# Where a batch's masks stand in the load queue, and where their conversions and sums stand on two engines

## The chip, the cores and the metric

The kernel runs on one core of one Trainium2 chip. The metric is device time in microseconds. The kernel before took 418.82, 419.46 and 419.88 us in three runs, a median of 419.46 us. A core has a matrix engine (TensorE, PE in the profile), a vector engine (VectorE, DVE), a scalar engine (ScalarE, ACT), GpSimd (POOL) and a queue that issues DMAs (SyncE, SP); ScalarE and GpSimd issue DMAs too. Each takes its own instructions in a fixed order.

## The reference, cut to what matters

```python
# first layer, each batch b of 8, 256 tokens of 1024 features
output = jnp.einsum('bsi,oi->bso', hidden_states, W) + b
sign = (2 * mask - 1).astype(hidden_states.dtype)
diff = jnp.einsum('bsi,bio->bso', hidden_states, sign)
x = x + output + diff * coeff[:, None, None]
# second layer: one shared W, and an adapter of rank 16 for each batch
base_out = jnp.einsum('bti,oi->bto', x, W) + b
lora_h = jnp.einsum('bti,bir->btr', x, A)
lora_out = jnp.einsum('btr,bro->bto', lora_h, Bm)
x = x + base_out + lora_out * SCALING
```

Each batch has an integer mask of 1024 x 1024. The first layer's weight of a batch is the shared weight, plus the identity (for the residual), plus the mask times 2c, minus c. All is float32.

## The kernel before

The eight batches are worked in two groups of four: first layer of batches 0 to 3, second layer of these four together, first layer of batches 4 to 7, second layer of those. Activations lie transposed (features on partitions).

**First layer.** A mask is loaded in eight pieces (`load`, L170) of 512 KB, each into a tile `w`, along with four tiles `x` of 256 KB. `build` (L219) turns a piece into a weight: a conversion on ScalarE (L231: times 2c, minus c) and a sum with the shared weight on VectorE (L234). Batches 3 to 7 (`SEVEN`) use a scheme with seven products of half-sized matrices instead of eight. `Seven.operands` makes its operands in 20 steps: the a11 and a12 pieces, two sums of token halves (t1, t2), then a22, a21 and the weight sums s1, s2 (L345), then t3, s3, s4, t4. `Seven.products` runs the seven products: X(a11), Y(a12), X(s2), Z(s1), X(s3), Z(s4), X(a22), each in two halves of 16 matmul instructions (L408), in PSUM banks X, Y, Z. Some results are read from PSUM with the bias on ScalarE (`with_bias`, four reads of L427), others are added on VectorE (`add`, L432). A bank that is accumulated further waits for its read. `Sevens.run_one` hands out operand steps about ten ahead of the products, so conversions and sums of the next batch fall among the reads and additions of the running one.

**Second layer.** `second_layer` runs seven outer products in the order A11, A12, S1, S2, S4, S3, A22 (`plan`). Each is again seven small products, on "leaves" of the weight: a11, s1, s2, a12, s3, a22, s4, of 256 KB each. Leaves are loaded by `load_leaves` on the SP queue. The leaf pool has seven buffers, so a leaf's load waits until an earlier leaf has been used. `run` (one outer product) calls `load_leaves` for the next outer product and starts its first small product X(a11) before the last two of its own. VectorE makes the right operands (T, L856, and their sums, L672 to L678), reads PSUM (L759) and adds the quarters of the result (L842); ScalarE copies the first reads (L757) and the adapters' results (L731). Work laid "beside" a run is taken in between: the sums of the next operands, the remaining leaves of the group's own weight, and `next_weights(n)`, which lets the first `n` operand steps of the next group's batch be built.

**Order.** A scheduler fixes the order of instructions on each engine when the program is built. `tc.issue_after(ins)` keeps what is recorded in it behind `ins` in that order. `behind(name)` does so with the latest instruction kept in `anchors` under that name: "leaves" is the last leaf load, "weights" the last weight sum or addition. `next_masks(n)` (L860) loads the first `n` pieces of the next group's first batch, here batch 4, behind the leaves that are queued at that point. The SP queue takes its loads in order.

Of the kernel before, what the change touches and what calls it, by code (L numbers as in the profile page):

```python
# [11 lines left out]
AF = mybir.ActivationFunctionType  # L12
# [12 lines left out]
def kernel(  # L25
# [38 lines left out]
    nc = tc.nc  # L64
# [42 lines left out]
    two_c = const.tile([P, B], F32, tag="two_c", name="two_c")  # L107
    nc.vector.tensor_scalar_mul(two_c, c_ps, 2.0)
    neg_c = const.tile([P, B], F32, tag="neg_c", name="neg_c")
# [26 lines left out]
    x_sb, weff, raw, weff_at = {}, {}, {}, {}  # L136
    anchors = {}
# [3 lines left out]
    pieces = [(0, None, c) for c in range(NC)]  # L141
    pieces += [(b, h, g) for b in range(1, B) for h, g in (by_seven if b in SEVEN else by_half)]

    def pair(name):
        return qpool.tile([P, 2, CG, OQ], F32, tag="q", name=name)

    def parts(k: int):

        return [slice(i, i + 1) for i in range(2)] if k < BY_HALF else [slice(0, 2)]
# [6 lines left out]
    def w0_of(k: int):  # L156
        b, h, g = pieces[k]
        if b == 0:
            return w0_sb[:, g, :].rearrange("p (h o) -> p h o", h=2)
        return w0_sb[:, g * CG : (g + 1) * CG, h * OH : (h + 1) * OH]  # L160
# [58 lines left out]
    def build(k: int):  # L219

        b, h, g = pieces[k]
        if k == 2 * NG:

            for c in range(NC):
                d = w0_sb[:, c, c * P : (c + 1) * P]
                with tc.issue_after(weff_at[k - 1].ins):
                    nc.vector.tensor_add(d, d, ident)
        w = weff[k]
        m = w.bitcast(I32)
        for i in parts(k):  # L230
            nc.scalar.activation(  # L231
                w[:, i], m[:, i], AF.Identity, bias=neg_c[:, b : b + 1], scale=two_c[:, b : b + 1]
            )
            weff_at[k] = nc.vector.tensor_add(w[:, i], w[:, i], w0_of(k)[:, i])  # L234
            anchors["weights"] = weff_at[k]

    loaded = 0
# [11 lines left out]
    def bank(name):  # L249
        return psum.tile([P, 2, T], F32, tag="ps", name=name)  # L250
# [67 lines left out]
    class Seven:  # L318
# [105 lines left out]
        def with_bias(self, i, v, ps):  # L424
            for j in range(TPH):
                ot = i * TPH + j
                nc.scalar.activation(  # L427
                    self.out(i, v)[:, j, :], ps[:, j, :], AF.Identity, bias=b0_sb[:, ot : ot + 1]
                )

        def add(self, i, v, ps):
            anchors["weights"] = nc.vector.tensor_add(self.out(i, v), ps, self.out(i, v))  # L432

        def products(self):

# [37 lines left out]

    OPERANDS_AHEAD = 10
    FREE_OPERANDS = 7
    def behind(what: str):
        return tc.issue_after(anchors[what].ins) if what in anchors else nullcontext()

    class Sevens:

# [200 lines left out]
    def second_layer(group: int, y, first, first_steps, second):  # L681
# [6 lines left out]
        left_leaf, right = {}, {}  # L688
# [7 lines left out]
        def product(ps, l, r, first=False, by_tile=False):  # L696
            order = [(c, j) for c in range(CG) for j in range(2)]
            if by_tile:
                order.sort(key=lambda cj: cj[1])

            with behind("products") if first else nullcontext(), behind("adapters"):
                for c, j in order:
                    anchors["inner"] = nc.tensor.matmul(  # L703
                        ps[:, j, :],
                        lhsT=l[:, c, j * P : (j + 1) * P],
                        rhs=r[:, c, :],
                        start=first and c == 0 and j == 0,
                        stop=False,
                        skip_group_check=True,
                    )  # L710
# [40 lines left out]
        def begin(n, name, r):  # L751
            banks[n] = bank(f"X_{group}_{n}")
            product(banks[n], left_leaf[name, "a11"], r.b[0, 0], first=True)

        def read(out, ps, other=None):
            if other is None:
                anchors["copies"] = nc.scalar.copy(out, ps)  # L757
                return anchors["copies"]
            own["reads"] = anchors["reads"] = nc.vector.tensor_add(out, ps, other)  # L759
            return anchors["reads"]  # L760

        def store(o, i, j, u, v, c=slice(0, CG), queue=nc.scalar):
            queue.dma_start(outT[GB * group + 2 * j + v, 2 * i + u][:, c], o)
# [3 lines left out]
        def run(n, name, r, seed, out, dest=None, beside=None, early=None, mid=None, late=None, then=None):  # L767

            leaf = {k: left_leaf.pop((name, k)) for k in ("a11", "s1", "s2", "a12", "s3", "a22", "s4")}
            other = seed or {uv: None for uv in UV}
            beside = beside or iter(())
            X = banks.pop(n)

            def done(uv):
                if dest:
                    store(out[uv], *dest, *uv)
                if then:
                    then(uv)  # L780

            read(out[0, 0], X, other[0, 0])
            Z = bank(f"Z_{group}_{n}")
            product(Z, leaf["s1"], r.t["t1"], first=True)
            if early:
                early()
            product(X, leaf["s2"], r.t["t2"])
            next(beside, None)
            read(out[0, 1], X, other[0, 1])
            Y = bank(f"Y_{group}_{n}")  # L790
            product(Y, leaf["a12"], r.b[1, 0], first=True)
            read(out[0, 0], Y, out[0, 0])
            done((0, 0))
            if mid:
                mid()
            if n + 1 == len(plan):
                finish(X, Z, leaf, r, other, out, dest, beside, done)
                return
            product(X, leaf["s3"], r.t["t3"])
            next(beside, None)  # L800
            read(out[1, 1], X, other[1, 1])
            read(out[1, 1], Z, out[1, 1])
            done((1, 1))
            load_leaves(plan[n + 1])
            begin(n + 1, plan[n + 1], right[plan[n + 1]])
            next(beside, None)
            product(X, leaf["a22"], r.t["t4"])
            read(out[1, 0], X, other[1, 0])
            done((1, 0))
            next(beside, None)  # L810
            if late:
                late()
            product(Z, leaf["s4"], r.b[1, 1])
            read(out[0, 1], Z, out[0, 1])
            done((0, 1))
            for _ in beside:
                pass
# [19 lines left out]
        def quads(name):  # L837
            two = [pair(f"{name}{u}_{group}") for u in range(2)]
            return {(u, v): two[u][:, v] for u, v in UV}

        def add(o, x):
            nc.vector.tensor_add(o, o, x)  # L842
# [5 lines left out]
        def outer_sum(n, x, y, name):  # L848


            big_t[n] = [
                tpool.tile([P, TPH, T], F32, tag="T", name=f"T{n}_{group}_{v}") for v in range(2)
            ]
            right[name] = Right(f"T{n}_{group}", big_t[n])
            for v in range(2):
                nc.vector.tensor_sub(big_t[n][v], x[v], y[v])  # L856
                yield
            yield from right[name].sums()

        def next_masks(n):  # L860

            with behind("leaves"):
                if group + 1 < NGROUP:
                    load_to((group + 1) * GB * 2 * NG + n)

        def next_weights(n):
            if group + 1 < NGROUP:
                while sevens[group + 1].made < n:
                    sevens[group + 1].begin(sevens[group + 1].made + 1)
                    yield  # L870


        def ordered(steps):

            while True:
                with behind("reads" if "reads" in own else "layer"):
                    if next(steps, True):
                        return
                yield
# [6 lines left out]
        for _ in ordered(first_steps):  # L886
# [6 lines left out]
            beside=chain(islice(s3, 1), ordered(second.sums()), islice(s3, 4), islice(t1, 2)),  # L893
# [5 lines left out]
        for uv in UV[1:]:  # L899
            add(c11[uv], e1[uv])  # L900
        t2 = ordered(outer_sum(2, b22, big_t[1], "S2"))
        next_masks(4)
        run(
            1, "A12", second, c11, c11,
            dest=(0, 0),
            beside=chain(t1, s3, islice(t2, 2)),
        )
        e5 = quads("e5")
        run(
            2, "S1", right["S1"], None, e5,  # L910
            beside=chain(t2, ordered(right["S4"].sums()), next_weights(2)),
            then=lambda uv: add(c12[uv], e5[uv]),
        )
        run(
            3, "S2", right["S2"], e1, e1,
            beside=ordered(outer_sum(3, b22, b12, "S3")),
            then=lambda uv: add(c12[uv], e1[uv]),
        )
        c21, c22 = quads("c21"), quads("c22")
# [4 lines left out]
            beside=chain(ordered(outer_sum(4, b21, big_t[2], "A22")), next_weights(3)),  # L924
# [169 lines left out]
```

## Time and profile before

| what | us |
|---|---|
| median of three runs | 419.46 |
| the profiled execution, its own time | 420.91 |
| its span, first to last instruction | 419.2 |
| TensorE busy | 404.0 |
| VectorE busy | 312.1 |
| ScalarE busy | 136.6 |
| TensorE's mean granted clock | 0.988 of full |

The span is what the profile divides into shares; the time of the execution is 1.7 us longer. In the profile, a wait is put down to what ended it. The four stages stand at about these places in the span: first layer of batches 0 to 3 until 115 us, second layer of group 0 until 219 us, first layer of batches 4 to 7 until 321 us, second layer of group 1 until the end. Transfers moved 99.56 MB, a mean of 237 GB/s.

### The profile page before, as it was taken

To read this page: it belongs to the slowest core of one execution; us is meant where nothing else is said; L and a number is where in the kernel's file an instruction comes from. 1 tells how busy PE (TensorE), PEld (TensorE's weight loads), DVE (VectorE), ACT (ScalarE), POOL (GpSimd) and SP (SyncE) were. 2 spreads that over 40 slices of the span, in tenths; PEclk is the share of its full clock that TensorE was granted. 3 is DMA by queue.
4 is the path that set the end of the run, shared out by engine and by line. 5 is a ranking of instruction groups with operands and counts; after the bars stand their busy time and mean duration, and the time that the engine had idled before them with its cause. 6 is when DMAs were issued, how large, how long until landed. Compare 5 with 4: busy or idle time off the path is not lost.

```text
span 419.2 us, 6762 instructions
## 1 busy us (share of the span) xinstructions
PE 404.0 (96%) x2554; PEld 360.7 (86%) x2554; DVE 312.1 (74%) x446; ACT 136.6 (33%) x221; POOL 43.0 (10%) x85
## 2 busy tenths in 40 slices
PE   8999999999999399999999899999999999999996
PEld 6888888899968378888889899999999688888885
DVE  3357688999706739997899999999913177898593
ACT  4443625681034001403045864623221330101100
POOL 0000252009750102000000000300000000000000
PEclk9999999999999869999999999999999999999999
DMA  8999999961998949556699948632112237545644
GB/s 291 403 401 398 401 407 412 404 242 43 368 363 276 367 141 299 164 148 210 192 343 406 373 153 306 215 122 62 27 52 65 88 125 231 172 151 160 213 155 151
DMA packets 42404, 99.56 MB, mean 237 GB/s; under 512 B 5636, under 2 KB 6404, under 8 KB 42372
## 3 DMA queue, kind: packets, MB, share of 16 engines
q1 hardware_dynamic: 32690, 76.17, 52.4%
q0 software_dynamic: 4928, 14.71, 9.3%
q10 hardware_dynamic: 4754, 8.26, 5.3%
q8 instruction: 20, 0.33, 0.3%
q14 instruction: 12, 0.10, 0.1%
HBM read 79.19 MB, written 19.92 MB: 236 GB/s over the span
## 4 chain that ended last, share of the span: by engine, by line
PE 77%; DMA 12%; DVE 6%; SPq 1%; ACT 1%; issue 1%; DVEq 0%; ACTq 0%
PE X L703 19%; PE X L408 14%; PE ps L267 13%; PE Z L703 8%; PE Z L408 8%; DMA w<-mask 7%; PE ps L292 4%; PE Y L703 4%; PE Y L408 3%; DMA l_S_a<-leaf_S_a 2%; PE G L721 2%; PE psh L738 2%; DMA w_sb<-w0T 2%; DMA outT<-c 2%; DVE c L842 1%; DVE e L759 1%
## 5 line engine op out<-in xcount | busy, mean ns | idle before, releaser
L231 ACT ACTIVATE w<-w,neg_c,two_c 128x1024 f32<-128x1024 int32 (+1 forms) x67 | 78.9, 1203 | 67.2 <-DMA w<-mask 55.4
L234 DVE TENSOR_TENSOR w<-w,w_sb 128x1024 f32<-128x1024 f32 (+1 forms) x67 | 77.1, 1173 | 25.4 <-ACT w L231 17.5
L267 PE MATMUL ps<-x,w 128*128 128x256 f32 x256 | 55.4, 379 | 0.0
L267 PEld LDWEIGHTS ps<-x,w 128*128 128x128 f32 x256 | 48.6, 190 | 6.6
L427 ACT ACTIVATE y<-X,b_sb 128x128 f32<-128x128 f32 x60 | 17.1, 366 | 58.2 <-PE X L408 58.2
L408 PE MATMUL X<-t,s 128*128 128x128 f32 x288 | 34.0, 276 | 2.0 <-ACT y L427 1.9
L842 DVE TENSOR_TENSOR c<-c,e 128x512 f32<-128x512 f32 x48 | 32.1, 684 | 4.6 <-ACT c L731 4.6
L408 PEld LDWEIGHTS X<-t,s 128*128 128x128 f32 x288 | 32.9, 192 | 2.4 <-ACT y L427 2.4
L731 ACT COPY c<-G 128x512 f32<-128x512 f32 x32 | 16.4, 599 | 49.1 <-PE G L721 33.2
L292 PE MATMUL ps<-x,w 128*128 128x256 f32 x128 | 28.4, 383 | 0.5 <-DVE w L234 0.5
L757 ACT COPY e<-X 128x512 f32<-128x512 f32 x16 | 9.4, 588 | 58.9 <-PE X L703 52.6
L759 DVE TENSOR_TENSOR c<-X,c 128x512 f32<-128x512 f32 (+1 forms) x26 | 16.6, 646 | 16.1 <-PE X L703 16.0
L292 PEld LDWEIGHTS ps<-x,w 128*128 128x128 f32 x128 | 24.6, 193 | 4.3 <-DVE w L234 0.9
L759 DVE TENSOR_TENSOR e<-Y,e 128x512 f32<-128x512 f32 x8 | 5.5, 689 | 25.8 <-PE Y L703 14.0
L703 PE MATMUL X<-T_t,l_S_s 128*128 128x256 f32 x96 | 22.8, 380 | 0.1
L408 PE MATMUL X<-t,w 128*128 128x128 f32 x192 | 22.4, 275 | 0.0
L408 PEld LDWEIGHTS X<-t,w 128*128 128x128 f32 x192 | 21.9, 192 | 0.0
L345 DVE TENSOR_TENSOR s<-w,w 128x1024 f32<-128x1024 f32 x18 | 21.7, 1218 | 0.1
L703 PEld LDWEIGHTS X<-T_t,l_S_s 128*128 128x128 f32 x96 | 18.2, 190 | 2.9 <-DVE e L759 0.5
L703 PE MATMUL X<-T,l_S_a 128*128 128x256 f32 x48 | 12.8, 410 | 7.2 <-DMA l_S_a<-leaf_S_a 7.2
L408 PE MATMUL Z<-t,s 128*128 128x128 f32 x160 | 18.8, 275 | 0.0
L408 PE MATMUL Y<-x,w 128*128 128x128 f32 x160 | 18.7, 275 | 0.0
(144 smaller groups left out, 672.0 us busy)
## 6 DMA issues: line engine op xcount, KB each, us to landing
w<-mask SPq DMA_DIRECT2D x61, 512.0 KB, 7.1
l_S_s<-leaf_S_s SPq DMA_DIRECT2D x32, 256.0 KB, 2.7
x<-xT SPq DMA_DIRECT2D x31, 256.0 KB, 7.0
outT<-c ACTq DMA_DIRECT2D x30, 256.0 KB, 3.0
l_A_s<-leaf_A_s SPq DMA_DIRECT2D x24, 256.0 KB, 2.7
l_S_a<-leaf_S_a SPq DMA_DIRECT2D x24, 256.0 KB, 3.2
w<-w1T SPq DMA_DIRECT2D x16, 256.0 KB, 7.2
leaf_A_s<-A_s POOLq DMA_DIRECT2D x12, 256.0 KB, 6.4
```

The costliest lines, as they stand in the source:

```text
L231: nc.scalar.activation(w[:, i], m[:, i], AF.Identity, bias=neg_c[:, b : b + 1], scale=two_c[:, b : b + 1])
L234: weff_at[k] = nc.vector.tensor_add(w[:, i], w[:, i], w0_of(k)[:, i])
L267: nc.tensor.matmul(ps[j // 2][:, j % 2, :], lhsT=w[:, c, j * P : (j + 1) * P], rhs=x_sb[b, g][:, c, :],  start=first and j % 2 == 0, stop= ...
L292: nc.tensor.matmul(ps[ot // 2][:, ot % 2, :], lhsT=w[:, h, j * P : (j + 1) * P], rhs=x_sb[0, c // CG][:, c % CG, :], start=c == 0 and ot % ...
L345: anchors["weights"] = op(s, self.w[x, a], self.w[y, a])
L408: anchors["products"] = nc.tensor.matmul(ps[:, j, :], lhsT=w[:, c, j * P : (j + 1) * P], rhs=r, start=first and a == 0 and c == 0 and j == ...
L427: nc.scalar.activation(self.out(i, v)[:, j, :], ps[:, j, :], AF.Identity, bias=b0_sb[:, ot : ot + 1])
L703: anchors["inner"] = nc.tensor.matmul(ps[:, j, :], lhsT=l[:, c, j * P : (j + 1) * P], rhs=r[:, c, :], start=first and c == 0 and j == 0, s ...
L731: nc.scalar.copy(dest[b // 2][u, b % 2], ps[b])
L757: anchors["copies"] = nc.scalar.copy(out, ps)
L759: own["reads"] = anchors["reads"] = nc.vector.tensor_add(out, ps, other)
L842: nc.vector.tensor_add(o, o, x)
```

## The change

Three things change. (1) `next_masks(4)` no longer stands ahead of the run of A12 but is split: two pieces of batch 4 after that run, that is behind S1's leaves, and the other two after the run of S1, behind S2's leaves. `next_weights(2)` moves from beside the run of S1 to beside that of S2. (2) `build` records the conversion of a mask behind the latest biased read (`anchors["bias"]`, set in `with_bias`). (3) `build` records the sum of a weight behind the latest addition of a product (`anchors["adds"]`, set in `add`). Where no such anchor is set yet (batches 0 to 2 and the beginning of 3), (2) and (3) do nothing.

```diff
         for i in parts(k):
-            nc.scalar.activation(
-                w[:, i], m[:, i], AF.Identity, bias=neg_c[:, b : b + 1], scale=two_c[:, b : b + 1]
-            )
-            weff_at[k] = nc.vector.tensor_add(w[:, i], w[:, i], w0_of(k)[:, i])
+            with behind("bias"):
+                nc.scalar.activation(
+                    w[:, i],
+                    m[:, i],
+                    AF.Identity,
+                    bias=neg_c[:, b : b + 1],
+                    scale=two_c[:, b : b + 1],
+                )
+            with behind("adds"):
+                weff_at[k] = nc.vector.tensor_add(w[:, i], w[:, i], w0_of(k)[:, i])
             anchors["weights"] = weff_at[k]
...
-                nc.scalar.activation(
+                anchors["bias"] = nc.scalar.activation(
                     self.out(i, v)[:, j, :], ps[:, j, :], AF.Identity, bias=b0_sb[:, ot : ot + 1]
                 )
...
-            anchors["weights"] = nc.vector.tensor_add(self.out(i, v), ps, self.out(i, v))
+            anchors["weights"] = anchors["adds"] = nc.vector.tensor_add(
+                self.out(i, v), ps, self.out(i, v)
+            )
...
         t2 = ordered(outer_sum(2, b22, big_t[1], "S2"))
-        next_masks(4)
         run(
             1, "A12", second, c11, c11,
             dest=(0, 0),
             beside=chain(t1, s3, islice(t2, 2)),
         )
+        next_masks(2)
         e5 = quads("e5")
         run(
             2, "S1", right["S1"], None, e5,
-            beside=chain(t2, ordered(right["S4"].sums()), next_weights(2)),
+            beside=chain(t2, ordered(right["S4"].sums())),
             then=lambda uv: add(c12[uv], e5[uv]),
         )
+        next_masks(4)
         run(
             3, "S2", right["S2"], e1, e1,
-            beside=ordered(outer_sum(3, b22, b12, "S3")),
+            beside=chain(ordered(outer_sum(3, b22, b12, "S3")), next_weights(2)),
             then=lambda uv: add(c12[uv], e1[uv]),
         )
```

More of the change, by code (lines that the diff above doesn't have):

```diff
@@ L142, with behind @@
     pieces += [(b, h, g) for b in range(1, B) for h, g in (by_seven if b in SEVEN else by_half)]
+    def behind(what: str):
+        return tc.issue_after(anchors[what].ins) if what in anchors else nullcontext()
     def pair(name):
@@ L475 @@
     FREE_OPERANDS = 7
-    def behind(what: str):
-        return tc.issue_after(anchors[what].ins) if what in anchors else nullcontext()
     class Sevens:
```

## The prediction

> **What bounds the kernel now.** I read the waits view first, then the chain of waits, then busy time by stretch, and last the timeline with the order of instructions of both kernels. TensorE is busy 404.0 of 419.2 us, so only its gaps and its slow stretches can be won. From the waits view (engine, line, awaited: us in total, times, longest):
> ```profile
> ACT w L231 <- DMA w<-mask: 55.4, 30, 15.1
> ...
> PE X L703 <- DMA l_S_a<-leaf_S_a: 7.2, 1, 7.2
> ...
> PE X L408 <- ACT y L427: 1.9, 1, 1.9
> ```
> Two waits of TensorE can be moved: 7.2 us for one leaf, 1.9 us for one biased read on ScalarE. ScalarE's own 55.4 us for masks costs nothing unless something is queued behind it. The chain of waits (start, us, what) shows both places:
> ```profile
> 137.65 9.68 DMA l_S_a<-leaf_S_a
> 147.33 0.14 issue
> 147.46 8.28 PE X L703 x24
> ...
> 226.57 6.38 DMA w<-mask
> 232.95 0.02 issue
> 232.97 1.24 ACT w L231
> 234.21 1.04 ACT y L427 x4
> 235.25 0.04 issue
> 235.30 3.84 PE X L408 x32
> ```
> First place: the leaf a11 of product S1 is issued at 137.65, behind four masks and four x tiles (132.6 to 137.6; 2 MB + 1 MB), and lands at 147.33. The 24 matmuls after it take 8.28 us, where 24 take 5.18 elsewhere in the chain (347.01). Second place: a bias read (L427) stands on ScalarE behind a conversion (L231) whose mask lands at 232.95, and the next matmul waits for the read. By stretch (columns: PE, PEld, DVE, ACT, POOL busy and count, clock, DMA share, GB/s):
> ```profile
> 137.65:147.46 9.81, 2.61 (x13) 1.98 (x12) 6.44 (x9) 0.00 (x0) 1.29 (x3) 0.77 1.02 390
> 147.46:155.74 8.28, 8.28 (x25) 6.83 (x26) 1.98 (x3) 0.59 (x1) 0.00 (x0) 0.65 0.37 91
> 155.74:176.55 20.81, 20.72 (x97) 17.89 (x95) 20.33 (x30) 6.29 (x7) 2.17 (x4) 1.00 0.78 246
> ...
> 218.90:246.10 27.20, 25.32 (x225) 25.11 (x224) 26.16 (x33) 18.50 (x26) 0.00 (x0) 1.00 0.94 364
> 246.10:271.10 25.00, 25.00 (x226) 25.00 (x225) 24.46 (x34) 14.70 (x25) 2.71 (x5) 1.00 0.62 215
> 271.10:296.50 25.40, 25.29 (x226) 25.10 (x226) 25.40 (x31) 7.96 (x19) 1.58 (x3) 1.00 0.30 95
> ```
> See the DMA share of 1.02 during the stall, the clock at 0.65 after it, and VectorE without a gap afterwards (20.33 of 20.81). The last three lines are batches 4, 5 and 6: 27.2, 25.0 and 25.4 us for the same matmuls. So the stall costs 7.2 + (8.28 - 5.18) = 10.3 us, and batches 4 and 6 hold 2.2 + 0.4 over the clean one: 12.9 us is the most there is.
>
> [...] idle from 140.3, clock 0.50 from 143 to 153, back 5.6 us after work resumed. The gap of 1.9 us left the clock at 1.00. [...]
>
> **The masks' move (L902, and next_weights(2) of L911).** It adds no instruction. In the built order SP now has S1's seven leaves, two masks with two x tiles, S2's leaves, two masks with two x tiles, S4's leaves. Leaf loads wait for a buffer: a11 of S1 for A11's last Z product (133.09 + 1.99, less the overlap: 135.0), then s1, s2, a12 for A12's products ending at 136.6, 138.3, 140.3. With the usual 2.6 to 3.2 us they land at about 138, 139.5, 141.2, 143. TensorE ends Y of A12 at 140.3; its operand T is ready at 139.9 (138.73 + 1.13). One leaf product is 1.73 us (x8 in the chain). The built order then gives: X of S1 140.3 to 142.0; half of Z(s1), whose operand ends at 142.3, to 143.2; X(s3) of A12 to 144.9; the other half 145.8; X(a22) 147.5; Z(s4) 149.3. Before, that Z(s4) ended at 157.5, and S1's X(s2) began at 159.0; now it begins at 149.3. TensorE is 9.7 us early, 8.2 of it in what VectorE follows.
>
> Then VectorE binds. From the read of that Z (157.51) to the read of S4's X (187.09 + 0.68) it works without a real gap: 37 tiles of 128x512 at 0.60 from start to start, five T tiles (L856) and two weight sums (L234) at 1.13 = 22.2 + 5.7 + 2.3 = 30.2 us. The built order has the same instructions, rearranged. From 149.3 they end at 179.5; one read (S2's X after a22, TensorE until 172.9) makes them wait 0.4, so 179.9. S4's X(s3), which needs the last read, begins at 180.0 instead of 188.2: 8.2 us early. After 188.2 TensorE is full for 30.7 us (188.2 to 218.9), SP's waits are for the same products, and all of it shifts.
>
> What can take some back is the masks' new place. The first pair is issued behind S1's s4 leaf (its buffer is free at 145.8) at 146.5 to 148.1, 1.5 MB. A lone mask lands after 4.42 us (207.44 in the chain); at 0.39 MB/us each further 512 KB adds 1.3, so S2's a11 behind it lands at 146.5 + 4.4 + 0.7 + 1.3 + 0.7 + 0.7 = 154.3, or 155.6 if two outT tiles go between. It is wanted at 154.5: 0 to 1.1 us. The second pair, issued at 158.4 after S2's s4, gives S4's a11 at 166.2 against 165.9: 0.3 to 0.5. Behind the leaf there is one VectorE wait of 1.0 (S2's X(s2) waits for a read at 164.2) that covers part. I take 0.7 for both together; the ends are 0 and 3, the latter if each block lands 1.5 late. Stage: 8.2 - 0.7 = 7.5 us. The conversions of these masks on ScalarE (4 of some 1.15) run at about 159 to 165, ahead of the G copies that follow them there at 178; their first two sums on VectorE move from S1's run to S2's (next_weights), inside the 30.2 us, and batch 4 wants them at 210. On SP the S2 leaves also wait for outT stores of A12, four in ScalarE's queue, landing 3.0 after issue: at 153 at the latest, where s1 of S2 is wanted at 159.7. The weights of batch 5 and on do not move on SP.
>
> **The holds (L231 and L234).** No instruction is added and no semaphore of another engine: only the order on ScalarE and VectorE changes, in batches 4 to 7. Count from a batch's first matmul, a product being 3.57 us: X 3.57, Y 7.15, X(s2) 10.7, Z(s1) 14.3, X(s3) 17.9, Z(s4) 21.4, X(a22) 25.0. In batch 4 the X(s2) read now comes first at 10.8 to 11.9, the first conversion after it, the Z read at 14.4 to 15.5, five conversions to 21.3, the last read at 25.0 to 26.1, two conversions to 28.4 (1.15 to 1.20 each). TensorE's X(s3) at 14.3 finds its bank read: the 1.9 us goes. The 0.2 us that batch 4 loses to VectorE at 228.3 stays. Batch 6's gap before 278.5, a read behind a mask conversion, goes too: 0.3.
>
> What is queued behind the held work: VectorE's sums for the next batch. The a11, a12 sums end at 14.2, 17.9, 19.0, 20.3; the read of X(s3) at 21.0, wanted at 21.4; a22, a21 at 22.0 and 23.8; s1, s2 at 25.4 and 26.9; the second pair, converted at 27.3 and 28.4, sums at 28.5 and 29.6, its s1, s2 at 31.4 and 33.0. The next batch wants the latter at 25.0 + 8.9 = 33.9. Slack 0.9 us in the tightest boundary (5 to 6), 0.4 on the X(s3) read. Masks for these are older: the latest of batch 5 that is converted here lands at 232.95, 14.0 after batch 4's start, wanted at 20.1. The trace of before does not show this order, so bounds: gain 2.6 at best, loss of 0.5 at each of three boundaries if 1 us of latency is missing. I take 2.1.
>
> **Sum.** 7.5 + 2.1 = 9.6 us. The profiled execution took 420.91 (span 419.2), so 411.3 for its like; the runs' median of 419.46 is 1.45 below it, and 9.6 less is 409.9.
>
> **Rivals.**
> A. The leaves of S2 and S4 come late by 1.5 us each and VectorE cannot hide it. For it: 390 GB/s is the limit in the stall, and S4's a11 has no spare time. Against: half the bytes of before stand ahead of either[...]. Gain 8.2 - 3 + 2.1 = 7.3 less some follow-on 0.6: 412.8.
> B. The holds gain nothing: the 1.9 us comes back as 0.5 us at three boundaries. For it: slack of 0.4 and 0.9 us, VectorE 24.5 busy of 25.0. Against: the sums have the same pace as before at batch 4. 7.5 - 1.5 = 6.0: 413.5.
> C. Slower: the holds chain VectorE to TensorE. Place: the second pair of a21, a22 at the turn of batches 5, 6 and 7, converted only after the last biased read. [...] It decides from 2.5 us a turn (3 x 2.5 = 7.5). For it: VectorE has 0.5 us to spare in batch 5 (24.46 of 25.00) and now waits for reads. Against: the built order has no further instructions there.
> D. The masks' move does nothing, as the leaves wait for something else. Their waits in the built order (buffer, an earlier load, stores long done) speak against: 417.4 with the holds alone.
>
> **Chances.** Forecast 0.60 (own range 407.3 to 411.8), A 0.17, B 0.12, C 0.08, D 0.03. Low end: 12.4 of the 12.9 us, 407.1. High end: A whole and B up to its figure, 413.5; this leaves out some of B, C, D and the tail of the first. Below 0.3% (1.3 us) a measurement of this kernel can't be told from no change. Faster 0.90 (forecast, A, B and part of D), same 0.02, slower 0.08.
>
> **What would show it.** Right: no TensorE wait for l_S_a above 1.2 us, clock 1.00 through 140 to 160, S1's X beginning by 141, VectorE without a gap from about 149 to 180, first matmul of batch 4 at 210.7 to 211.6, batches 4 to 7 at 25.0 to 25.4 each, no PE wait for ACT y. Wrong: a wait of X or Z (L703) for S2 or S4 leaves above 1.5 us, a clock below 1.00 after 140, VectorE gaps before the weight sums with PE waiting for DVE s (L345) in batches 5 to 7.

## The result and the profile after

The changed kernel took 419.67 us (median of 14 runs, 417.74 to 421.15), the kernel before beside it 419.77 (14 runs). The ratio is 0.999 with a 95% interval of 0.9967 to 1.0012: no change, where 409.9 had been predicted. The profiled execution took 420.21 us with a span of 418.5, against 420.91 and 419.2.

The first part went as forecast: in the trace S1's X begins at 140.05 (prediction 140.3) and Z(s4) of A12 ends at 149.5 (149.3), so TensorE was 9.5 us early. The waits of TensorE show where that went (engine, line, awaited: us in total, times, longest). Lines have moved: L714 is the second layer's product, L419 the first layer's, L770 the PSUM read on VectorE, L206 the mask load, L210 the x load, L704 the leaf load.

```profile
PE X L714 <- DMA l_S_a<-leaf_S_a: 5.4, 2, 4.7
...
PE X L714 <- DVE e L770: 1.0, 1, 1.0
PE X L714 <- DVE c L770: 1.0, 1, 1.0
PE X L419 <- DVE s L356: 0.7, 1, 0.7
```

The wait for l_S_a is still there, 5.4 us instead of 7.2, and there are two of them. The wait for y on ScalarE (1.9 us before) is gone. The chain of waits of the changed kernel (start, us, what):

```profile
146.06 3.99 DMA l_S_s<-leaf_S_s
...
150.12 9.26 DMA l_S_a<-leaf_S_a
159.38 0.14 issue
159.51 5.78 PE X L714 x16
...
167.63 6.50 DMA l_S_a<-leaf_S_a
174.13 0.14 issue
174.27 1.96 PE X L714 x8
...
188.67 5.45 PE X L714 x24
```

The leaf that is late is now S2's a11: issued at 150.12, landed after 9.26 us at 159.38. The 16 matmuls behind it take 5.78 us, where 24 take 5.45 further down. S4's a11 is late too (6.50 us), and S4's X(s3), forecast for 180.7 (180.0 and the 0.7 for the masks), begins at 188.67; before it was 188.26. The whole gain was given back within 40 us.

SyncE's queue shows what stands ahead of that leaf (start, us, instruction):

```profile
146.06 0.32 SPq L704 DMA_DIRECT2D l_S_s<-leaf_S_s  x1
146.49 0.37 SPq L206 DMA_DIRECT2D w<-mask  x1
146.91 0.42 SPq L210 DMA_DIRECT2D x<-xT  x1
147.43 0.37 SPq L206 DMA_DIRECT2D w<-mask  x1
147.86 0.74 SPq L210 DMA_DIRECT2D x<-xT  x1
150.12 0.33 SPq L704 DMA_DIRECT2D l_S_a<-leaf_S_a  x1
```

Two masks and two x tiles, 1.57 MB: the first mask landed at 153.39 (6.91 us after its issue), the last x tile at 158.10. The stretches show the rest (from:to and length, busy us of PE, PEld, DVE, ACT, POOL with counts, TensorE clock, DMA share, GB/s):

```profile
140.05:149.51 9.46, 9.09 (x41) 7.46 (x41) 7.26 (x11) 0.58 (x1) 0.00 (x0) 1.00 0.74 233
149.51:154.85 5.34, 5.34 (x25) 4.37 (x23) 5.14 (x7) 0.59 (x1) 1.16 (x3) 1.00 1.01 366
154.85:159.51 4.66, 0.00 (x1) 0.03 (x1) 4.43 (x8) 0.59 (x1) 1.00 (x2) 0.72 1.03 401
159.51:165.29 5.78, 5.78 (x17) 4.79 (x18) 0.00 (x0) 0.00 (x0) 0.00 (x0) 0.64 0.44 165
...
219.40:244.45 25.05, 25.05 (x225) 25.05 (x224) 25.05 (x32) 11.10 (x19) 0.00 (x0) 1.00 1.00 376
244.45:269.83 25.38, 25.28 (x226) 25.09 (x225) 25.25 (x38) 13.58 (x24) 4.28 (x8) 1.00 0.69 220
269.83:295.82 25.99, 25.28 (x226) 25.09 (x225) 23.98 (x28) 13.59 (x24) 0.00 (x0) 1.00 0.26 86
```

The idle 4.66 us (third line) have the same signature as the stall before: DMA share 1.03, 401 GB/s, then a clock of 0.64. It is the old stall, one product later. The last three lines are batches 4, 5 and 6, each from its first matmul to that of the next. Batch 4 gained 2.15 us (27.20 before) as forecast; batch 5 lost 0.37 (25.01 before) and batch 6 lost 0.60 (25.39 before) where 0.3 was to be won.

The theories tested: **T1**, the stall moved with the masks; against it **T2**, other traffic (the writes of results to outT on ScalarE's queue, and the stores of the S3 leaves on GpSimd's) makes the leaf late; **T3**, only its late issue does; **T4**, VectorE would have eaten the gain anyway. The holds were taken apart separately.

### The profile page after: what moved, and what is told of

The parts are those of the page before. It is cut to its first block, busy times and chain, and to the rows that moved or that the text cites. A ratio compares the mean times of both kernels' runs of the same rounds, so it can differ in the third digit from the quotient of the medians.

```text
span 418.5 us, 6751 instructions
## 1 busy us (share of the span) xinstructions
PE 404.1 (97%) x2554; PEld 359.8 (86%) x2554; DVE 312.8 (75%) x446; ACT 136.4 (33%) x221; POOL 42.8 (10%) x85
## 4 chain that ended last, share of the span: by engine, by line
PE 84%; DMA 9%; DVE 4%; SPq 1%; issue 1%; DVEq 0%
PE X L714 22%; PE X L419 15%; PE ps L278 13%; PE Z L714 10%; PE Z L419 8%; PE Y L714 5%; PE ps L303 4%; DMA l_S_a<-leaf_S_a 4%; PE Y L419 3%; PE G L732 2%; DMA x<-xT 2%; PE psh L749 2%; DMA w_sb<-w0T 2%; DVE w L245 1%; DMA w<-mask 1%; DMA l_S_s<-leaf_S_s 1%
## 5 line engine op out<-in xcount | busy, mean ns | idle before, releaser
L419 PE MATMUL X<-t,s 128*128 128x128 f32 x288 | 34.1, 275 | 0.7 <-DVE s L356 0.7
L419 PEld LDWEIGHTS X<-t,s 128*128 128x128 f32 x288 | 33.0, 192 | 0.9 <-DVE s L356 0.9
L770 DVE TENSOR_TENSOR e<-Y,e 128x512 f32<-128x512 f32 x8 | 5.5, 689 | 25.8 <-PE Y L714 14.0
L714 PE MATMUL X<-T_t,l_S_s 128*128 128x256 f32 x96 | 22.8, 380 | 1.0 <-DVE e L770 1.0
L770 DVE TENSOR_TENSOR c<-X,c 128x512 f32<-128x512 f32 (+1 forms) x26 | 16.6, 645 | 8.7 <-PE X L714 8.7
L419 PE MATMUL X<-t,w 128*128 128x128 f32 x192 | 22.5, 276 | 0.1
L419 PEld LDWEIGHTS X<-t,w 128*128 128x128 f32 x192 | 21.9, 192 | 0.3 <-DVE y L443 0.3
L714 PEld LDWEIGHTS X<-T_t,l_S_s 128*128 128x128 f32 x96 | 18.2, 190 | 3.9 <-DVE e L770 1.4
L419 PE MATMUL Z<-t,s 128*128 128x128 f32 x160 | 18.8, 275 | 0.0
L419 PE MATMUL Y<-x,w 128*128 128x128 f32 x160 | 18.7, 275 | 0.0
L419 PE MATMUL X<-x,w 128*128 128x128 f32 x160 | 18.7, 275 | 0.0
```

What stands on the lines that cost most here:

```text
L419: anchors["products"] = nc.tensor.matmul(ps[:, j, :], lhsT=w[:, c, j * P : (j + 1) * P], rhs=r, start=first and a == 0 and c == 0 and j == ...
L714: anchors["inner"] = nc.tensor.matmul(ps[:, j, :], lhsT=l[:, c, j * P : (j + 1) * P], rhs=r[:, c, :], start=first and c == 0 and j == 0, s ...
```

## The experiments

**Each half alone.** One kernel moves the masks without the holds, one has the holds with the masks as before.

```diff
# masks alone
-            with behind("bias"):
+            with nullcontext():
...
-            with behind("adds"):
+            with nullcontext():
# holds alone
         t2 = ordered(outer_sum(2, b22, big_t[1], "S2"))
+        next_masks(4)
...
-        next_masks(2)
...
-        next_masks(4)
```

> The changed kernel without its two holds: only the masks (and next_weights) are moved. Theory T1 (the wait moved with the masks, from S1's a11 to S2's a11, and gives back what was won): S2's a11 again lands about 9 us after its issue, TensorE idles about 4.7 us there and batch 4 begins at about 219.5, so about 420.5 us, against 419.8 for the kernel before. The prediction's own theory (masks' move worth 7.5): batch 4 begins at 211.4 and the time is about 412. Rival T4 (the holds on the second layer's side, by a changed order on VectorE, ate the gain): batch 4 begins at 211 to 213 as soon as they are gone. The 1.9 us wait for y in batch 4 must be back under every theory.

> The holds alone, masks and next_weights as in the kernel before. S1's a11 stalls as before (idle 7.2 us, batch 4 at 218.9). If the holds give what the stretches of the changed kernel show (batch 4 gains 2.15, batch 6 loses 0.97): span shorter by 1.2 to 1.4, about 418.4 us. If batch 6's loss comes from the later start of the masks' chain rather than from the holds, it is absent here: shorter by 2.1 to 2.5, about 417.4. If the holds gain nothing: 419.8.

The masks alone took 420.51 us, ratio 1.001 (0.9985 to 1.0035): nothing, and the stall is there without the holds (S2's a11 8.00 us, TensorE idle 3.48). The holds alone took 417.83, ratio 0.993 (0.989 to 0.997), with batches 4 to 6 at 25.05, 25.38 and 25.01. So the masks' move is the part that failed. T4 in the form "the holds ate it" is out. (Idle times and landings here and below are read from one profiled execution of each kernel.)

**The pair one product later, and one mask behind each group of leaves.**

```diff
# a pair behind S2's leaves, a pair behind S4's
-        next_masks(2)        # ahead of the run of S1
...
-        next_masks(4)        # ahead of the run of S2
+        next_masks(2)
...
+        next_masks(4)        # ahead of the run of S4
# one mask and x tile behind the leaves of S1, S2, S4 and S3
-        next_masks(2)
+        next_masks(1)
...
-        next_masks(4)
+        next_masks(2)
...
+        next_masks(3)
...
+        next_masks(4)
```

In both, `next_weights` follows the masks.

> The changed kernel with both mask pairs one product later: two masks and their x behind S2's leaves, two behind S4's. T1 (masks ahead of the leaf): S2's a11 lands within 5 us of its issue and TensorE does not wait for it above 1.5 us; the first pair now stands ahead of S4's a11, which is needed with VectorE's work in between, so at most 2 to 3 us come back; batch 4 begins at 211 to 214 and the time is 411 to 415. T2 (not the masks but the stores and the outT writes that run at 147 to 160 make that leaf late): S2's a11 still lands 7 us or more after its issue, PE idles over 3 us, batch 4 at 216 or later, 417 or more. T4 (VectorE would have eaten the gain anyway): no PE wait for leaves, and batch 4 at 217 or later all the same.

> The same four masks, one with its x tile behind each of the leaf groups of S1, S2, S4 and S3. T1 with the price read in the changed kernel (each 0.77 MB block costs about 2 us of the 16 DMA engines): S2's a11 lands 6 to 7 us after its issue instead of 9.3, TensorE waits 1 to 2.5 us, its clock stays up, and batch 4 begins at 211 to 213.5, so 410 to 413.5 us. T2 (stores): as in the changed kernel less 1 us, PE idle over 3 us, 417 to 419. T3 ([...]the late issue behind s4, makes the leaf late): the issue is as late as before, and the wait stays at 4 us or more.

412.45 us, ratio 0.979 (0.973 to 0.984), and 412.39, ratio 0.978 (0.973 to 0.984). With nothing ahead of it S2's a11 took 3.18 us (148.62 to 151.80), with one mask and x tile 5.73 (148.20 to 153.93); TensorE waited for neither. The same S3 stores were issued in both (151.93 to 156.61 and 151.52 to 156.20), but in the first the leaf had landed before any of them, and in the second it landed when only two had been issued, so these runs don't rule T2 out; the next one does. What is left lies at S4's a11, which now has masks ahead of it: a wait of 1.45 us with the pair, of 3.06 with one. T3 is not separated by these runs: with fewer loads in between, the leaf was also issued 1.5 to 1.9 us earlier.

**The stores out of the way.** In the changed kernel the four stores of the S3 leaves (1.05 MB) were moved past the stretch.

```diff
-            beside=chain(t1, s3, islice(t2, 2)),
+            beside=chain(t1, islice(t2, 2)),
...
-            beside=chain(t2, ordered(right["S4"].sums())),
+            beside=chain(t2, ordered(right["S4"].sums()), s3),
```

> The changed kernel with the sums (and so the four stores, 1.05 MB) of the S3 leaves moved from beside the run of A12 to the end of what lies beside the run of S1, so that they leave the stretch in which the first mask pair and S2's a11 are under way. Masks as in the changed kernel. If the masks ahead of the leaf in the queue are what matters (T1a): S2's a11 still lands 7.5 to 9.5 us after its issue, TensorE idles 3 to 4.7 us, about 418 to 420 us. If the write traffic beside them is half of it (T2): S2's a11 lands within 6.5 us, TensorE idles under 2 us, the clock stays at 1.00, and 411 to 414 us come out. The loss of 1 us in batch 6 is looked at again here: if it belongs to the holds, it is back (26.0 us for batch 6); if it was one execution's DMA, 25.0 to 25.2.

417.51 us, ratio 0.992 (0.988 to 0.995). It fell between the two forecasts. The chain of that kernel:

```profile
150.91 6.95 DMA l_S_a<-leaf_S_a
157.85 0.14 issue
157.99 5.39 PE X L714 x16
...
185.78 7.13 PE X L714 x24
```

The leaf took 6.95 us and TensorE idled 2.50, against 3.48 to 4.66 in the three kernels that have the same masks and the stores in this stretch. What the DMA queues moved between the leaf's issue and its landing (packets, MB, share of the 16 engines), first in the changed kernel (3.55 MB in 9.26 us), then here (2.57 MB in 6.95 us):

```profile
q1 hardware_dynamic: 962, 2.07, 62.0%
q10 hardware_dynamic: 418, 0.76, 21.3%
q0 software_dynamic: 205, 0.70, 18.7%
```

```profile
q1 hardware_dynamic: 870, 1.93, 79.1%
q10 hardware_dynamic: 353, 0.63, 23.8%
```

By what was under way, q1 has SyncE's loads, q10 the outT writes and q0 the stores, which are gone in the second. So the stores, which moved up from 159 to 164 into 151 to 156 when VectorE became early, were 1.0 to 2.2 us of the stall. T2 as the sole cause is out: 2.50 us of idling remain without them. The masks, the outT writes and the late issue are the larger part. The clock fell all the same (to 0.50 for 3.42 us, 16 matmuls in 5.39 us; see the last section). The later S3 sums made TensorE wait 1.7 us for VectorE at S4's X(s3), and behind that wait the clock fell a second time (0.50 for 3.41 us, 24 matmuls in 7.13 us instead of 5.45), so the time of this kernel understates what the stores cost.

**The first leaf ahead of the pair.** What changes is the leaf's place in the queue, ahead of four loads instead of behind them; the order on VectorE is the same.

```diff
                 left_leaf[name, n] = t
+                if n == "a11" and name in masks_in:
+                    masks_in.pop(name)()
...
-        next_masks(2)
+        masks_in.update(S2=lambda: next_masks(2), S4=lambda: next_masks(4))
...
-        next_masks(4)
```

> The changed kernel with one edit: each pair of masks is queued behind the first leaf (a11) of S2 and of S4 instead of ahead of it. The same bytes in about the same stretch, the same order on VectorE. T1a (place in the queue): S2's a11 lands within 4 us of its issue, S4's a11 too, no wait of TensorE for l_S_a above 0.5 us; the second leaf s1, now the one behind the masks, is wanted 5 us later and may cost 0 to 1.5 us (seen as Z waiting for l_S_s). Batch 4 begins at 210.7 to 212.5, and the time is 410 to 412 us. T1b (the amount of traffic in that stretch, whatever its order): S2's a11 lands 7 us or later after its issue and 415 us or more come out.

414.96 us, ratio 0.986 (0.983 to 0.990). Its waits (L717 is here the product):

```profile
PE Z L717 <- DMA l_S_s<-leaf_S_s: 3.0, 2, 2.1
...
PE X L717 <- DMA l_S_a<-leaf_S_a: 0.3, 1, 0.3
```

S2's a11 landed after 4.10 us and costs nothing, with the same bytes close by: here the place in the queue decided which leaf was late. (The place sets the issue too: this a11 was issued at 148.31, 1.8 us earlier than in the changed kernel, so T3 is not separated here either.) But the next leaf, s1, is now the late one (2.1 us at S2, 0.9 at S4). It is needed 5 us after a11, and that was 2 us too soon for the pair.

**No masks where TensorE and VectorE are tight.** One mask behind S1's leaves, one behind S4's, two behind S3's.

```diff
-        next_masks(2)
+        next_masks(1)
...
-        next_masks(4)        # ahead of the run of S2
...
+        next_masks(2)        # ahead of the run of S4
...
+        next_masks(4)        # ahead of the run of S3
```

Here too `next_weights` follows the masks.

> Masks spread as one behind S1's leaves, one behind S4's, two behind S3's; their first operand steps accordingly later. In the run with one behind each group, one mask ahead of S2's a11 cost TensorE nothing and one ahead of S4's a11 cost 3.1 us. T1: both leaves in time, TensorE full from 149.5 to about 180 apart from VectorE; S4's X(s3) begins at 180.0 to 181.5 (VectorE's chain as worked out in the prediction: 180.0), batch 4 at 210.7 to 212, about 410 to 411.5 us, provided that the last two masks, issued at about 185 to 188, are built in time; if they are not, batch 4 itself is longer by 1 to 3 us. T4 (VectorE cannot carry it): X(s3) at 182 or later with no wait for a leaf.

411.62 us, ratio 0.980 (0.976 to 0.984). The profiled execution was the fastest of its four (411.17, span 409.5). The chain:

```profile
149.77 1.73 PE X L714 x8
151.50 1.73 PE Y L714 x8
153.22 5.18 PE X L714 x24
...
178.01 1.22 DVE w L245
179.23 0.61 DVE c L770
...
179.88 5.45 PE X L714 x24
```

No DMA stands in it from 149.8 to 179.9, and S4's X(s3) begins at 179.88; the prediction had 180.0 without late masks. T4 is out: VectorE's chain was sized rightly, and the 8.2 us were there to be had.

**The holds taken apart.** Masks as before; once only the conversions held, once only the sums.

```diff
# conversions held
-            with behind("adds"):
+            with nullcontext():
# sums held
-            with behind("bias"):
+            with nullcontext():
```

> Masks as in the kernel before, and of the two holds only that of the conversions behind the biased reads. Both holds together made it 2.5 us faster (417.83 against 420.31). If the bias hold is what removes the waits for y in batches 4 and 6: again 417.5 to 418.2, batch 4 at 25.0 to 25.3 us. If the hold of the sums contributes half: 419.0 to 419.3. If the hold of the sums alone takes something back: below 417.5.

> Masks as in the kernel before, and of the two holds only that of the weight sums behind the additions on VectorE. The bias hold alone gave 0.9963 of before (418.71 us; batches 4 and 6 at 25.05 and 25.02 us), both holds 0.993. If the bias hold is all of the gain: batch 4 at 27.0 to 27.2 again with the wait for y, batch 6 at 25.4, and 419.5 to 420. If the hold of the sums has a part of its own: 418.7 to 419.2, with batch 4 below 26.5. If it costs something: above 420.5.

418.71 us, ratio 0.9963 (0.9944 to 0.9983), and 420.02, ratio 0.9982 (0.996 to 1.0004). Once conversions are held, holding the sums changes nothing: this kernel and the one with both holds have the same order of instructions on every engine. Their batches agree (25.05, 25.37 and 25.02 against 25.05, 25.38 and 25.01), and the 417.83 and 418.71 us are two measurements of one program. The sums' hold alone left a wait for y of 0.67 us in batch 4 and no difference in time that can be told. Its batch 4 was 25.99 us long, not the 27.0 to 27.2 expected; with no hold at all (the masks alone) the wait was 1.16 and batch 4 took 26.47. So that wait varies from trace to trace where the conversions are not held, and 25.99 is no sign of a gain by the sums.

**The loss in batches 5 and 6.** In the changed kernel VectorE waits 1.17 us at 271.61 for an x tile of batch 7, issued behind six masks and landing after 7.29 us; eight adapter loads of GpSimd (issued 260.4 to 264.9) run beside. Here they are moved one batch later, once in the changed kernel, once in the spread of one, one and two.

```diff
-            if b % GB == 2 and group:
-                load_adapters(group, y[1][0][:, 0, :1])
+            if b % GB == 3 and group:
+                load_adapters(group, y[2][0][:, 0, :1])
```

> The changed kernel with nothing but the adapter loads of group 1 moved one batch later. The masks' place is that of the changed kernel, so TensorE idles 3 to 5 us at S2's a11 as before. Batch 6, 26.0 us in the changed kernel: 25.0 to 25.1 if the adapter loads beside the six masks are the cause of the late x tile, 25.9 if they are not. Time 418.6 to 419.0 in the first case, 419.6 in the second.

> The masks spread as one, one and two (behind the leaves of S1, S4 and S3) and the adapters of group 1 loaded one batch later, beside batch 7 instead of beside batch 5's end. The spread alone gave 411.62 us with batch 6 at 25.6 us and one wait of 0.35 there. If the eight adapter loads are what holds up the mask and x tiles of batch 7: batch 6 at 25.0 to 25.1, and 0.4 to 0.7 us less, 410.9 to 411.2. If not: 411.6. If the adapters are late for the second layer of group 1 there (wanted 35 us later): slower by up to 3 us.

In the changed kernel: 419.12 us, ratio 0.996 (0.9937 to 0.9983), and these are batches 4, 5 and 6:

```profile
220.13:245.18 25.05, 25.05 (x226) 25.05 (x225) 25.05 (x32) 10.76 (x19) 0.00 (x0) 1.00 0.99 367
245.18:270.19 25.01, 25.01 (x227) 25.01 (x225) 25.01 (x34) 13.59 (x24) 0.00 (x0) 1.00 0.62 216
270.19:295.20 25.01, 25.01 (x226) 25.01 (x225) 24.13 (x32) 13.58 (x24) 4.29 (x8) 1.00 0.32 101
```

Both losses are gone (25.38 and 25.99 before this edit), so in the changed kernel the adapters' loads, with the small copies on VectorE that precede them, were the cause (which of the two, this edit doesn't tell); S2's a11 still took 9.36 us. In the spread the edit brought 411.29 us, ratio 0.975 (0.971 to 0.979), no different from 411.62. Batch 6 stayed at 25.63 there, as a read for y stands behind three weight sums on VectorE, which the expectation had not seen.

**One sum less before X(s3).** In that kernel the first weight sum of batch 4 leaves VectorE's chain.

```diff
-            beside=chain(ordered(outer_sum(3, b22, b12, "S3")), next_weights(1)),
+            beside=ordered(outer_sum(3, b22, b12, "S3")),
```

> The spread of one, one and two masks with the adapters one batch later, and the first weight sum of batch 4 (1.13 us on VectorE) taken out of the stretch before S4's X(s3) and put beside the run of S3. In the spread TensorE has no leaf to wait for and X(s3) begins at 179.9 to 180.7 after a wait of 1.16 us for VectorE. If VectorE's chain is the bound there, as the prediction has it (30.2 us from 149.3, of which two weight sums 2.3): the wait goes, X(s3) begins at 178.7 to 179.5, and 1.1 us come out, 410.2. If the bound lies in TensorE or in a leaf: X(s3) as before, 411.3. If the later first sum delays batch 4: slower than 411.5.

X(s3) began at 178.71, as VectorE's chain says, but the time was 411.59 us, ratio 0.979 (0.976 to 0.982): no gain. Batch 4 gives most of it back in three waits of TensorE of 0.25 to 0.34 us for its sums s and for y. This is where the time now stands; the spread and its two variants are the fastest found, and they can't be told apart.

## Why the prediction was wrong, point by point

- **The stall at S1's a11 goes.** Right: X of S1 begins at 140.05, Z(s4) ends at 149.5, and TensorE waits for no leaf there.
- **VectorE binds from 149.3 and lets X(s3) begin at 180.0.** Right where it could be seen: 179.88 in the spread, and 1.13 us of work taken out moved it by 1.17.
- **"I take 0.7 for both together; the ends are 0 and 3" (the masks' new place).** This step failed. In the changed kernel X(s3) is 8.7 us later than 180.0. The terms: TensorE idle 4.66 at S2's a11, 2.3 of slow clock behind it (5.78 us against 3.46 for 16 matmuls at full clock), 0.8 at S4's a11, and 2.0 in two waits for VectorE reads behind these late products; less the 1.16 that X(s3) waits for VectorE in the spread too.
- **The landing itself.** Forecast 154.3 to 155.6, measured 159.38. The pair was priced as a lone mask of 4.42 us and 0.39 MB/us after it. The first mask took 6.91, and the leaf was issued at 150.12 instead of about 148.5: in the trace its issue is released by the landing of S1's s4 (3.99 us after issue). "Stores long done" looked at what the leaf loads wait for, and left out the write traffic that would move up with VectorE: 0.70 MB of S3 stores beside 0.76 MB of outT writes, of 3.55 MB that moved between the leaf's issue and its landing. 1.0 to 2.2 us of the idling went with the stores. How the rest is divided between the pair's own bytes, the outT writes and the late issue was not separated.
- **"Half the bytes of before stand ahead of either"**, the argument against rival A. Half the bytes is right (1.57 MB against 3.1), but the leaf's flight hardly shrank, 9.26 us against 9.68; it was only issued earlier ahead of its use, 4.7 us against 2.6. And the clock fell, to 0.50 for 6.83 us. Rival A named the right mechanism and was priced at 1.5 us a leaf.
- **"clock 1.00 through 140 to 160"**: this was the author's estimate. In the changed kernel the clock fell to 0.50 at 156.90. In the trace of before it had fallen at 143.03, 2.8 us after TensorE had gone idle (140.26), and came back at 153.27, 5.8 us after work had resumed (147.46), and the gap of 1.9 us that ended at 235.30 left it at 1.00. How long a gap may be was not shown by these two; the last section has more of them.
- **The holds: 2.1.** Right alone: batches 4 to 6 gained 2.15, -0.37 and 0.38, together 2.2. In the changed kernel 1.2 remained, since batch 6 lost 0.60: six masks, the x tile and the adapters' loads meet, a meeting that the prediction did not look for. The sign of rivals B and C, TensorE waiting for VectorE's s, did appear (0.71 us in batch 6 of the changed kernel), but behind the late x tile, and it went with the adapters' move. The fear for the held sums was unfounded: beside the held conversions that hold changes no order.
- **The sum.** 9.6 us were forecast as the fall. The spread, which is another kernel, has a median 8.3 us lower (411.62 against 419.90). Most of the gain existed; the place given to the masks did not leave it standing.

## What to carry to other kernels

Here the loads that were moved in a shared queue took their delay along: the flight of the leaf behind them was 9.68 us before and 9.26 after. Before pricing the new place at nothing, work out for the next load behind it when it is issued, how much stands ahead of it and beside it, and how long it can wait, with everything that will run earlier once the old stall is gone (stores included). Where two loads can't both be early, put the bulk transfer where the next urgent one is farthest off, in pieces. One piece of 0.79 MB ahead of S2's leaf cost TensorE nothing here; two, with the stores beside them, cost 5 to 8 us in idling and slow clock; and one piece ahead of S4's leaf, which had less time to spare, cost 3.06 us.

## What was not expected of the hardware

The clock did not follow the length of a gap alone. After a gap of 3.06 us (one mask behind each group) it stayed at 1.00; after one of 2.50 us (stores moved) it fell to 0.50 for 3.4 us, and later in the same kernel it fell again after one of 1.71 us. The traces suggest that what counts is how a gap lies on a fixed grid. But for the first and last microseconds, the half-clock stretches are whole steps of 3.41 us: one step in the kernel with the masks alone, one at each of the two places in that with the stores moved, two (6.83, from 156.90 to 163.73) in the changed kernel, three (10.24, from 143.03 to 153.27) in the kernel before. The stretches of full clock fit the same steps: from 153.27 until it fell at the end, at 419.51, are 266.24 us or 78 steps in the kernel before, and from 163.73 to 419.73 are 256.00 us or 75 in the changed one. Cut on that grid, the 2.50 us gap with the step behind it, and the 1.71 us gap with the step behind it (columns as in the stretches above):

```profile
155.31:158.72 3.41, 0.92 (x5) 0.68 (x5) 3.02 (x5) 0.58 (x1) 0.00 (x0) 1.00 1.00 376
158.72:162.14 3.42, 3.42 (x10) 2.70 (x9) 1.07 (x2) 0.00 (x0) 0.00 (x0) 0.50 0.30 101
```

```profile
182.62:186.03 3.41, 1.71 (x19) 0.97 (x18) 3.41 (x5) 1.94 (x4) 0.00 (x0) 1.00 0.53 173
186.03:189.44 3.41, 3.41 (x9) 2.70 (x9) 1.47 (x3) 0.12 (x1) 0.00 (x0) 0.50 0.20 77
```

and the 3.06 us gap, which the grid cuts into 1.52 and 1.54:

```profile
161.92:165.33 3.41, 1.89 (x9) 1.33 (x7) 3.41 (x6) 0.00 (x0) 0.00 (x0) 1.00 0.89 309
165.33:168.75 3.42, 1.88 (x9) 1.71 (x10) 2.45 (x3) 1.24 (x1) 0.00 (x0) 1.00 0.34 113
```

Steps at full clock, by TensorE's idle time in them: those with 1.42 (170.55 to 173.97 in the changed kernel), 1.52 and 1.54 (above) and 1.77 us (231.77 to 235.19 in the kernel before, most of the wait for y) were not followed by half clock; those with 1.70 and 2.49 (above), 2.05 (153.49 to 156.90 in the changed kernel) and 2.77 us (139.61 to 143.03 in the kernel before) were. An estimate from these eight is that it turns at about half a step, 1.7 us. In the traces of the changed kernel and the one before, the clock changed only where such a step ends, and with the masks alone and the stores moved the stretches of half clock are whole steps. So the slow part behind a stall was not of one length: 16 matmuls behind the same masks took 5.18, 5.78 and 6.47 us (masks alone, changed kernel, adapters later) instead of 3.46.

A bulk load ahead of S2's a11 delayed it by about its bytes: its flight was 3.18 us with none, 5.73 with one mask and x tile, and 8.00 to 9.36 with two (6.95 without the stores). At the 401 GB/s measured in the stall, 0.79 MB are 2.0 us, 1.57 MB are 3.9 and the 0.70 MB of stores 1.7, an estimate that comes near each of these. It is no more than that, since part of each load had moved before the leaf was issued.
